# The last image's gate stage in a four-layer convolution kernel: channel mean by norm groups, one DFT row spread to all partitions, normed image made ahead

## The chip, the cores and the metric

The kernel runs on one core of one Trainium2 chip. A core has five engines, each with its own instruction queue that is worked in order: TensorE (PE; its weight loads are listed apart as PEld), VectorE (DVE), ScalarE (ACT), GpSimd (POOL) and SyncE (SP, which here only issues transfers). On-chip memory has 128 partitions; matrix products are written to PSUM. The metric is the device time of one execution in microseconds (us). All data are fp32.

## The reference

The input is x of shape (4, 256, 56, 56). Four layers follow each other, each of the form x + layer(group norm of x), with 32 groups of 8 channels. Layers 0 and 2 are involutions (a 7x7 filter made per pixel), layer 1 is a pair of 3x3 convolutions, layer 3 is a gate by Fourier transforms. Only layer 3 is touched:

```python
cf = jnp.fft.fft2(x, axes=(-2, -1)).real.mean(axis=(-2, -1))
cf = jax.nn.sigmoid(cf @ W.T + b)
x_cft = x * cf[:, :, None, None]
sf = jnp.fft.fft2(x.mean(axis=1, keepdims=True), axes=(-2, -1)).real.mean(axis=1)
x_sft = x * sf[:, None, :, :]
return x_cft + x_sft
```

The x in these lines is already the group norm of x; call it xn. The mean of a two-dimensional DFT is the value at the origin, so cf is a sigmoid of W times xn at pixel (0, 0), one number per channel. sf is the real part of the DFT of the channel mean m of xn, one 56x56 plane per image: cos·m·cos − sin·m·sin. The output is x + xn·(cf + sf).

## The kernel before

Channels lie on partitions, in two blocks cb = 0 and 1 of 128 channels; an image block is a tile `xs` of 128 partitions by 3136 pixels. The kernel is written as one program; `in_order` fixes each engine's order to the order in which the instructions are written. Layers 0 and 2 share `involution_layer`. For each of the 8 units (image b, block cb) it runs a tap stage (`tap_matrices`: TensorE L471, evacuated to `kt` by VectorE at L489 and by ScalarE at L482) and then 7 column stages (`apply`: TensorE L513, combined by ScalarE L528 and VectorE L533, and added into the image by VectorE L540). Smaller jobs are hung into the tap stage as `hooks` by number, or behind a column stage as `early` and `late` lists.

Layer 3 rides on layer 2. For images 0 to 2 its work is hung into later units: `channel_mean`, `gate_factors`, and `gate_chunk` (on GpSimd, 14 chunks an image). For the last image there is no later unit for block 1, so the end of `involution_layer` does this in turn:

- the last column's statistics (L844), then `norm_steps`: L194 aggregates, TensorE L197 averages the means over groups, L200 to L205 make the variance, TensorE L208 averages it, L138 and GpSimd's power L139 make `rstd`, L212 makes `shift`;
- `channel_mean(3, 1)`: L574 takes pixel (0, 0); L593 and L596 multiply the image by rstd/256 (32 equal columns, seven chunks of 448 pixels in four column groups), ScalarE L604 adds the shift's mean, L607 writes the mean to DRAM and L608 reads it back as 56 rows on 56 partitions (`m2_of`);
- `gate_factors(3)`: L616 loads w3, L623 and the sigmoid L630 make `cf`, L639 and L649 make the first half of the DFT in `half` (128 partitions x 56);
- `last_gates`: for each of seven chunks of 8 image rows, eight products L700 make sf on all 128 partitions at once. The weights are one column of `half` repeated 128 times, the moving operand is the 56-column table `cs2_sb`. ScalarE L710 makes xn in one of three `gx` buffers, VectorE L713 multiplies it by (sf + cf), GpSimd (block 0) or VectorE (block 1) adds it to `xs` at L715, and L716 stores it, from GpSimd's queue or from SP's.

`dead(b, cb, at, n)` gives scratch room in an image block that is no longer needed; for the last image it is a spare block. `two_banks` hands out PSUM in four pairs of banks, in rotation; `one_bank` is the first of a pair.

Of the kernel before, what the change touches and what calls it, by code (L numbers as in the profile page):

```python
# [10 lines left out]
F32 = mybir.dt.float32  # L11
AF = mybir.ActivationFunctionType
ALU = mybir.AluOpType
# [3 lines left out]
P = 128  # L17
B, C, H, W = 4, 256, 56, 56
NB = C // P
# [7 lines left out]
CR = 8  # L27
NCHUNK = H // CR
# [37 lines left out]
def run(g):  # L66
    for _ in g:
        pass
# [3 lines left out]
def net_kernel(  # L72
# [111 lines left out]
    norms = [[[norm_sb[:, i, b, k, :] for k in range(2)] for b in range(B)] for i in range(4)]  # L184
# [57 lines left out]
    def involution_layer(layer, xin, xout, red, span, sb, xs_of, ahead=None, pending=None):  # L242

        with ExitStack() as es:
# [29 lines left out]
            z_sb = wpool.tile([P, G // 2, ZN], F32, name="z_sb")  # L274
# [67 lines left out]
            strip_sb = wpool.tile([P, HS, QX], F32, name="strip_sb")  # L342
# [214 lines left out]
            def gx_tile():  # L557
                return work.tile([P, CR * W], F32, name="gx", bufs=3)

            def dead(b, cb, at, n):  # L560

                if b < B - 1:
                    return xs_of[b, cb][:, at : at + n]
                if None not in xs_of:
                    xs_of[None] = new_block()
                return xs_of[None][:, at : at + n]
# [121 lines left out]
                nc.gpsimd.dma_start(ov[b, cb][:, at], xs)  # L688
                yield

            def last_gates(b):

                rstd, shift = norms[3][b]
                for j in range(NCHUNK):
                    at = slice(j * CR * W, (j + 1) * CR * W)
                    sf = one_bank()[:, : CR * W]

                    for r in range(CR):
                        y = j * CR + r
                        nc.tensor.matmul(  # L700
                            sf[:, r * W : (r + 1) * W],
                            half[:, y : y + 1].to_broadcast([P, P]),
                            cs2_sb,
                            start=True,
                            stop=True,
                        )
                    for cb in range(NB):
                        xs = xs_of[b, cb][:, at]
                        xn = gx_tile()
                        nc.scalar.activation(  # L710
                            xn, xs, AF.Identity, bias=shift[:, cb : cb + 1], scale=rstd[:, cb : cb + 1]
                        )
                        nc.vector.scalar_tensor_tensor(xn, sf, cf_of[b][:, cb : cb + 1], xn, ALU.add, ALU.mult)  # L713
                        eng = nc.vector if cb == 1 else nc.gpsimd
                        eng.tensor_tensor(xs, xs, xn, ALU.add)  # L715
                        (nc.sync if cb == 1 else nc.gpsimd).dma_start(ov[b, cb][:, at], xs)  # L716


            def step(g):
# [63 lines left out]
            for u, (b, cb) in enumerate(units):  # L783
                hooks = hooks0 if u == 0 else {}
                if prev is not None:
                    pb, pc, st, last_sums = prev
                    hooks.setdefault(1, []).append(last_column(last_sums))
                    place(hooks, norm_of(layer + 1, pb, pc, st), (2, 6, 7, 11, 12, 13))
                    if layer == 2 and u < 3:
                        g = norm_of(2, B - 1, u - 1, pending[1][u - 1])  # L790
                        place(hooks, g, (19, 20, 22, 23, 25, 26))
                    if layer == 2:
                        place(hooks, channel_mean(pb, pc), (13, 17))
                        if pc == 1:
# [48 lines left out]
                def column_sums(tx, st=st, img=img):  # L843
                    nc.vector.bn_stats(st[:, tx, :], img[:, :, tx * TX : (tx + 1) * TX])  # L844

                if ahead is not None and u == len(units) - 1:
                    late[0].append(ahead)

                for tx in range(NTX):
                    for f in early[tx]:  # L850
                        f()
                    apply(b, cb, kt, tx, xws[u * NTX + tx])
                    next_windows()
                    next_strip()
                    if tx > 0:
                        column_sums(tx - 1)
                    for f in late[tx]:
                        f()
                if layer == 0 or b + 1 < B:
                    (nc.gpsimd if layer == 0 else nc.sync).dma_start(xout[b][cb], xs_of[b, cb])  # L860
                prev = b, cb, st, column_sums
            b, cb, st, last_sums = prev
            last_sums(NTX - 1)
            run(norm_of(layer + 1, b, cb, st))
            if layer == 2:
                factors = gate_factors(b)
                run(channel_mean(b, cb))
                for _ in range(4):
                    next(factors)
                last_gates(b)  # L870
            in_order(since)
# [596 lines left out]
```

## Time and profile before

| | before |
|---|---|
| time, median of 3 | 1877.03 us (1874.28 to 1877.57) |
| profiled span | 1872.6 us |
| PE busy | 1709.5 us (91%), 24030 instructions |
| DVE busy | 1433.3 us (77%) |
| ACT busy | 748.8 us (40%) |
| POOL busy | 432.2 us (23%) |
| last image write by L540 ends | 1820.6 us |
| first POOL add L715 starts | 1842.66 us |
| last POOL store L716 is issued by | 1865.13 us |

The profile is one execution. A line of a group reads: line, engine, operation, output<-inputs with their shapes (for a product the first pair is rows by columns of the weights), count | busy us, mean ns of one | idle us of the engine just before, and who released it. A line of the timeline reads: start in us, duration in us, engine, line, operation, count, and in brackets the idle time before it with its releaser. An fp32 product shows as two matmul records. PEclk is the clock that TensorE was granted, as a share of full speed. Matmul ends are modelled, so a busy PE is not PE at its peak.

### The profile page before, as it was taken

To read this page: it belongs to the slowest core of one execution; us is meant where nothing else is said; L and a number is where in the kernel's file an instruction comes from. 1 tells how busy PE (TensorE), PEld (TensorE's weight loads), DVE (VectorE), ACT (ScalarE), POOL (GpSimd) and SP (SyncE) were. 2 spreads that over 40 slices of the span, in tenths; PEclk is the share of its full clock that TensorE was granted. 3 is DMA by queue.
4 is the path that set the end of the run, shared out by engine and by line. 5 is a ranking of instruction groups with operands and counts; after the bars stand their busy time and mean duration, and the time that the engine had idled before them with its cause. 6 is when DMAs were issued, how large, how long until landed. Compare 5 with 4: busy or idle time off the path is not lost.

```text
span 1872.6 us, 55573 instructions
## 1 busy us (share of the span) xinstructions
PE 1709.5 (91%) x24030; PEld 1509.6 (81%) x24030; DVE 1433.3 (77%) x2823; ACT 748.8 (40%) x1657; POOL 432.2 (23%) x615
## 2 busy tenths in 40 slices
PE   5999999999759999999999999997999898898866
PEld 3888888888748988898899889885877777778865
DVE  5687777876678988898888988865767777777763
ACT  2445445454423222232223212114666565565532
POOL 2323433244210000000000000000000581681672
PEclk9999999999979999999999999998999999999995
DMA  3445544453533111110111210223533764773652
GB/s 97 150 146 177 153 120 140 152 153 111 160 121 100 42 60 61 61 67 36 62 58 57 73 35 33 89 76 89 174 107 132 231 193 147 222 215 105 177 147 76
DMA packets 65589, 215.72 MB, mean 115 GB/s; under 512 B 13564, under 2 KB 20528, under 8 KB 61504
## 3 DMA queue, kind: packets, MB, share of 16 engines
q1 hardware_dynamic: 44448, 141.62, 24.1%
q0 software_dynamic: 14848, 65.85, 10.9%
q10 hardware_dynamic: 6048, 4.68, 0.8%
q8 instruction: 190, 3.11, 0.7%
q14 instruction: 55, 0.45, 0.1%
HBM read 76.24 MB, written 49.16 MB: 67 GB/s over the span
## 4 chain that ended last, share of the span: by engine, by line
PE 65%; DVE 21%; DMA 5%; POOL 3%; issue 3%; ACT 2%; SPq 1%; POOLq 0%; ACTq 0%; DVEq 0%
PE mm L1242 20%; PE ps L513 14%; DVE kt L489 12%; PE mm L1160 10%; PE ps L471 7%; PE mm L1131 6%; PE ps L381 4%; DMA xw<-xw 3%; PE ps L433 2%; DVE un L533 2%; PE ps L700 1%; ACT hp L452 1%; PE ps L596 1%; DVE st L844 1%; DMA xs<-in_x_dram 1%
## 5 line engine op out<-in xcount | busy, mean ns | idle before, releaser
L513 PE MATMUL ps<-kt,xw 126*32 126x48 f32 (+1 forms) x12544 | 383.5, 236 | 56.9 <-DMA xw<-xw 21.3
L513 PEld LDWEIGHTS ps<-kt,xw 126*32 126x32 f32 (+1 forms) x12544 | 344.2, 122 | 102.4 <-issue 48.1
L471 PE MATMUL ps<-hp,z_sb 64*126 64x133 f32 x6144 | 389.0, 282 | 19.2 <-DVE kt L489 7.0
L471 PEld LDWEIGHTS ps<-hp,z_sb 64*126 64x126 f32 x6144 | 370.7, 189 | 34.1 <-DVE kt L489 8.7
L489 DVE TENSOR_TENSOR kt<-ps,zb_sb 126x798 f32<-126x798 f32 x384 | 357.9, 978 | 43.6 <-PE ps L471 43.1
L1242 PE MATMUL mm<-v,u_sb 128*128 128x280 f32 (+1 forms) x1728 | 384.9, 384 | 3.3 <-DVE v L1067 3.3
L1242 PEld LDWEIGHTS mm<-v,u_sb 128*128 128x128 f32 x1728 | 327.6, 190 | 57.8 <-DVE v L1067 3.6
L482 ACT ACTIVATE kt<-ps,zb_sb 126x133 f32<-126x133 f32 x768 | 224.0, 441 | 179.4 <-PE ps L471 179.4
L1160 PE MATMUL mm<-v,u_sb 128*128 128x252 f32 (+1 forms) x936 | 211.2, 386 | 12.6 <-DVE v L1051 12.6
L1160 PEld LDWEIGHTS mm<-v,u_sb 128*128 128x128 f32 x936 | 177.2, 190 | 42.9 <-issue 12.6
L533 DVE SCALAR_TENSOR_TENSOR un<-ps,par_sb,un 128x240 f32<-128x240 f32 x224 | 98.4, 457 | 103.1 <-ACT un L526 98.8
L533 DVE SCALAR_TENSOR_TENSOR un<-ps,s,un 128x240 f32<-128x240 f32 x224 | 102.3, 457 | 92.9 <-ACT un L528 88.7
L1279 POOL DMA_DIRECT2D x<-xs x24 | 13.1, 546 | 684.9 <-DVE xs L1278 539.5
L1227 ACT ACTIVATE res<-xs,shift,norm_sb 128x1120 f32<-128x1120 f32 (+1 forms) x24 | 30.2, 1260 | 235.2 <-DVE xs L1278 119.7
L538 POOL TENSOR_TENSOR xs<-un,xs 128x240 f32<-128x240 f32 x112 | 72.4, 665 | 224.2 <-DVE un L533 224.1
L382 ACT COPY xw<-ps 126x896 f32<-126x896 f32 x112 | 101.5, 907 | 49.6 <-PE ps L381 39.2
L381 PE MATMUL ps<-ident_sb,strip_sb 128*126 128x128 f32 x784 | 111.4, 282 | 1.6 <-DVE kt L489 0.8
L526 ACT ACTIVATE un<-ps,par_sb 128x240 f32<-128x240 f32 x112 | 50.1, 448 | 138.6 <-PE ps L513 136.7
L1131 PE MATMUL mm<-xs,u_sb 128*128 128x126 f32 (+1 forms) x792 | 98.3, 277 | 1.3 <-DVE xs L1094 1.0
L528 ACT ACTIVATE un<-ps,bn_t,s 128x240 f32<-128x240 f32 x112 | 60.1, 538 | 97.8 <-PE ps L513 93.7
L139 POOL TENSOR_TENSOR norm_sb<-norm_sb,mhalf 128x1 f32<-128x1 f32 x32 | 19.2, 602 | 341.7 <-DVE norm_sb L138 341.7
L1131 PEld LDWEIGHTS mm<-xs,u_sb 128*128 128x128 f32 x792 | 94.3, 191 | 2.7 <-issue 1.4
(194 smaller groups left out, 1973.0 us busy)
## 6 DMA issues: line engine op xcount, KB each, us to landing
xw<-xw SPq DMA_DIRECT2D x168, 252.0 KB
xw<-xw SPq DMA_DIRECT2D x224, 126.0 KB
xw<-xw POOLq DMA_DIRECT2D x56, 252.0 KB, 4.7
xs<-x SPq DMA_DIRECT2D x24, 560.0 KB
x<-xs POOLq DMA_DIRECT2D x8, 1568.0 KB, 7.9
xs<-x SPq DMA_DIRECT2D x8, 1568.0 KB
xs<-in_x_dram SPq DMA_DIRECT2D x6, 1568.0 KB
x<-xs SPq DMA_DIRECT2D x6, 1568.0 KB
```

Of the source, the lines that this page charges most:

```text
L381: nc.tensor.transpose(ps[:Q, k * P : (k + 1) * P], flat[:, k * Q : (k + 1) * Q], ident_sb)
L382: nc.scalar.copy(xw[:, :NSB, :], ps[:Q, : NSB * P].rearrange("q (n c) -> q n c", n=NSB))
L471: nc.tensor.matmul(ps[:Q, i, k * NT : (k + 1) * NT], z_sb[i * R : (i + 1) * R, cb * GB // 2 + gp, z0 : z0 + Q], hp[i * R : (i + 1) * R, py ...
L482: nc.scalar.activation(kt[:, g0 + i, pb, :, k], ps[:Q, i, k * NT : (k + 1) * NT], AF.Identity, bias=zb_sb[:, cb * GB + g0 + i, p0 + k : p0 ...
L489: nc.vector.tensor_tensor(kt[:, g0 : g0 + 2, pb], ps[:Q, :, : PB * NT].rearrange("q i (k t) -> q i t k", k=PB), zb_sb[:, cb * GB + g0 : cb ...
L513: nc.tensor.matmul(v[m * j : m * j + m, i, :, k * TP : (k + 1) * TP], xw[:, window(ty), m * j : m * j + m], kt[:, ng * j : ng * j + ng, :, ...
L528: nc.scalar.activation(part, o[0], AF.Identity, bias=bn["t4"][:, cb : cb + 1], scale=bn["s4"][ng][:, 0, cb : cb + 1])
L533: nc.vector.scalar_tensor_tensor(part, o[e], s, part, ALU.mult, ALU.add)
L538: nc.gpsimd.tensor_tensor(dst, u, dst, ALU.add)
L1131: nc.tensor.matmul(ps[:, co * m : (co + 1) * m], u[ci][:, co * P : (co + 1) * P], v2[:, e, : n // 2, ci * WT : (ci + 1) * WT], start=(ci = ...
L1160: nc.tensor.matmul(ps, u1_sb[:, ci, dy, k, co * P : (co + 1) * P], v[:, k, dy * NB + ci : (dy + n - 1) * NB + ci + 1 : NB, :], start=(j == 0),
L1242: nc.tensor.matmul(ps, u2_sb[:, ci, dy, k, co * P : (co + 1) * P], v[:, k, dy * NB + ci : (dy + n - 1) * NB + ci + 1 : NB, :], start=(j == 0),
```

## The change

Only the last image is treated differently. For its block 1:

- `last_mean` takes the channel mean without transfers. For each of the 56 image columns x, a product with weights `xs[:, :, x]` (128 channels x 56 rows) and 16 moving columns of the averaging table gives the mean of each group of 8 channels, with the image row on the partition. These sums don't need the norm, which is applied afterwards: `rstd` of each group is spread over the partitions by one product, the sums are multiplied by it (`parts`) and reduced over the groups, and the mean of `shift` is added. The result is written straight to `m2_of[1]`.
- `norm_steps` is interleaved with it: the 56 products stand first in TensorE's order, the norm's two products behind them.
- `gate_factors(3)` starts at hook 20 of the last tap stage, so that w3 is loaded there.
- `last_normed` makes xn for the whole image ahead of the gates, for block 0 in the buffer of h, for block 1 in three `gx` buffers and in room that is free by then.
- `last_gates` makes sf once by one product (56x56), spreads its rows by a mask into `rows` (partition y holds row y in slot y mod 8, zeros elsewhere), and one product a chunk with a selecting weight brings the chunk's eight rows to all 128 partitions. `last_ones` makes mask and selector from the identity at hook 22.
- for block 1, VectorE multiplies by (sf + cf + 1/rstd), and ScalarE adds −shift/rstd, which gives x + xn·(cf + sf) without a VectorE addition.

```diff
+            def last_ones():
+                by = ident_sb[:, : CR * CR]
+                for i, axes in enumerate(("p (j r) -> p r j", "p (j r) -> p j r")):
+                    last_xn[i] = dead(B - 1, NB - 1, 6 * CR * W + 128 + i * CR, CR)
+                    nc.vector.tensor_reduce(last_xn[i], by.rearrange(axes, r=CR), mybir.AxisListType.X, ALU.add)
+            def last_normed(b, cb):
...
+                for j, xn in enumerate(pieces):
+                    last_xn[j, cb] = xn
+                    nc.scalar.activation(xn, xs_of[b, cb][:, j * n : (j + 1) * n], AF.Identity,
+                        bias=shift[:, cb : cb + 1], scale=rstd[:, cb : cb + 1])
+                    yield
+            def last_mean(b, bank):
+                cb, ng = NB - 1, P // 8
+                xs = xs_of[b, cb].rearrange("p (h w) -> p w h", w=W)
+                rstd, shift = (t[:, cb : cb + 1] for t in norms[3][b])
+                by = gavg_sb.rearrange("p (g i) -> p i g", i=8)[:, 0, :]
...
+                for x in range(W):
+                    nc.tensor.matmul(means[:, x // m, x % m, :], xs[:, x, :], by, start=True, stop=True)
+                yield
+                nc.tensor.matmul(bank[:H, 1 : 1 + ng], rstd.to_broadcast([P, H]), by, start=True, stop=True)
+                scales = dead(b, cb, 4 * CR * W + NB * C, 32)[:H]
+                yield
+                nc.tensor.matmul(
+                    bank[:H, 1 + ng : 2 + ng], shift.to_broadcast([P, H]), cmean[:, 0:1], start=True, stop=True)
+                nc.vector.tensor_scalar(first_of[b][:, cb : cb + 1], xs[:, 0, 0:1], rstd, shift, ALU.mult, ALU.add)
+                nc.vector.tensor_scalar_mul(scales[:, :ng], bank[:H, 1 : 1 + ng], 8.0 / C)
+                parts = dead(b, cb, 2 * CR * W, 2 * CR * W)[:H].rearrange("y (i x g) -> y i x g", i=2, g=ng)
+                nc.vector.tensor_tensor(parts, means,
+                    scales[:, :ng].unsqueeze(1).unsqueeze(1).to_broadcast([H, 2, m, ng]), ALU.mult)
+                nc.vector.tensor_copy(scales[:, ng : ng + 1], bank[:H, 1 + ng : 2 + ng])
+                nc.vector.tensor_reduce(
+                    m2_of[cb].rearrange("y (i x) -> y i x", i=2), parts, mybir.AxisListType.X, ALU.add)
+                nc.vector.tensor_scalar_add(m2_of[cb], m2_of[cb], scales[:, ng : ng + 1])
+                yield
             def last_gates(b):
...
+                nc.vector.reciprocal(inv, rstd[:, 1:2])
+                nc.vector.tensor_add(cfx, cf_of[b][:, 1:2], inv)
+                nc.vector.scalar_tensor_tensor(back, shift[:, 1:2], -1.0, inv, ALU.mult, ALU.mult)
+                ps = one_bank()
+                nc.tensor.matmul(ps[:H, :W], half, cs2_sb, start=True, stop=True)
+                rows = dead(b, NB - 1, 0, CR * W)[:H]
+                nc.vector.tensor_tensor(
+                    rows.rearrange("y (r w) -> y r w", r=CR),
+                    ps[:H, :W].unsqueeze(1).to_broadcast([H, CR, W]),
+                    last_xn[0][:H].unsqueeze(2).to_broadcast([H, CR, W]), ALU.mult)
                 for j in range(NCHUNK):
                     at = slice(j * CR * W, (j + 1) * CR * W)
                     sf = one_bank()[:, : CR * W]
-                    for r in range(CR):
-                        y = j * CR + r
-                        nc.tensor.matmul(sf[:, r * W : (r + 1) * W],
-                            half[:, y : y + 1].to_broadcast([P, P]), cs2_sb, start=True, stop=True)
+                    nc.tensor.matmul(sf, last_xn[1][:H, j : j + 1].to_broadcast([H, P]), rows, start=True, stop=True)
                     for cb in range(NB):
-                        xs = xs_of[b, cb][:, at]
-                        xn = gx_tile()
-                        nc.scalar.activation(
-                            xn, xs, AF.Identity, bias=shift[:, cb : cb + 1], scale=rstd[:, cb : cb + 1])
-                        nc.vector.scalar_tensor_tensor(xn, sf, cf_of[b][:, cb : cb + 1], xn, ALU.add, ALU.mult)
-                        eng = nc.vector if cb == 1 else nc.gpsimd
-                        eng.tensor_tensor(xs, xs, xn, ALU.add)
-                        (nc.sync if cb == 1 else nc.gpsimd).dma_start(ov[b, cb][:, at], xs)
+                        xs, xn = xs_of[b, cb][:, at], last_xn[j, cb]
+                        f = cfx if cb == 1 else cf_of[b][:, cb : cb + 1]
+                        nc.vector.scalar_tensor_tensor(xn, sf, f, xn, ALU.add, ALU.mult)
+                        if cb == 0:
+                            nc.gpsimd.tensor_tensor(xs, xs, xn, ALU.add)
+                            nc.gpsimd.dma_start(ov[b, cb][:, at], xs)
+                        else:
+                            nc.scalar.activation(xs, xn, AF.Identity, bias=back)
+                            nc.sync.dma_start(ov[b, cb][:, at], xs)
...
+                        elif pb == B - 1:
+                            factors = gate_factors(pb)
+                            place(hooks, factors, (20,))
+                            hooks.setdefault(22, []).append(last_ones)
...
-            run(norm_of(layer + 1, b, cb, st))
+            if layer == 0:
+                run(norm_of(layer + 1, b, cb, st))
             if layer == 2:
-                factors = gate_factors(b)
-                run(channel_mean(b, cb))
-                for _ in range(4):
+                run(last_normed(b, 0))
+                bank = one_bank()
+                mean, norm = last_mean(b, bank), norm_steps(st, lambda: bank, 3, b, cb)
+                next(mean)
+                for _ in range(5):
+                    next(norm)
+                next(mean)
+                next(norm)
+                next(mean)
+                normed = last_normed(b, cb)
+                for _ in range(2):
+                    next(normed)
+                next(factors)
+                run(normed)
+                for _ in range(2):
                     next(factors)
                 last_gates(b)
```

More of the change, by code (lines that the diff above doesn't have):

```diff
@@ L689, in gate_chunk @@
                 yield
+            last_xn = {}
+            def last_ones():
[4 more added lines that the diff above has]
+            def last_normed(b, cb):
+                rstd, shift = norms[3][b]
+                n = CR * W
+                if cb == 0:
+                    h = new_h()
+                    pieces = [h[:, j * n : (j + 1) * n] for j in range(NCHUNK)]
+                else:
+                    z = z_sb.rearrange("p g z -> p (g z)")
+                    pieces = [z[:, k * n : (k + 1) * n] for k in range(2)]
+                    pieces += [strip_sb.rearrange("p h w -> p (h w)")[:, :n], dead(b, cb, n, n)]
+                    pieces = [gx_tile() for _ in range(NCHUNK - len(pieces))] + pieces
+                for j, xn in enumerate(pieces):
+                    last_xn[j, cb] = xn
+                    nc.scalar.activation(
+                        xn,
+                        xs_of[b, cb][:, j * n : (j + 1) * n],
+                        AF.Identity,
+                        bias=shift[:, cb : cb + 1],
+                        scale=rstd[:, cb : cb + 1],
+                    )
+                    yield
@@ new lines, in last_mean @@
+            def last_mean(b, bank):
[3 more added lines that the diff above has]
+                by = gavg_sb.rearrange("p (g i) -> p i g", i=8)[:, 0, :]
+                m = W // 2
+                pair = two_banks()
+                means = pair[:H, :, : m * ng].rearrange("y i (x g) -> y i x g", g=ng)
+                for x in range(W):
[5 more added lines that the diff above has]
+                nc.tensor.matmul(
+                    bank[:H, 1 + ng : 2 + ng], shift.to_broadcast([P, H]), cmean[:, 0:1], start=True, stop=True
+                )
+                nc.vector.tensor_scalar(first_of[b][:, cb : cb + 1], xs[:, 0, 0:1], rstd, shift, ALU.mult, ALU.add)
+                nc.vector.tensor_scalar_mul(scales[:, :ng], bank[:H, 1 : 1 + ng], 8.0 / C)
+                parts = dead(b, cb, 2 * CR * W, 2 * CR * W)[:H].rearrange("y (i x g) -> y i x g", i=2, g=ng)
+                nc.vector.tensor_tensor(
+                    parts,
+                    means,
+                    scales[:, :ng].unsqueeze(1).unsqueeze(1).to_broadcast([H, 2, m, ng]),
+                    ALU.mult,
+                )
+                nc.vector.tensor_copy(scales[:, ng : ng + 1], bank[:H, 1 + ng : 2 + ng])
+                nc.vector.tensor_reduce(
+                    m2_of[cb].rearrange("y (i x) -> y i x", i=2), parts, mybir.AxisListType.X, ALU.add
+                )
+                nc.vector.tensor_scalar_add(m2_of[cb], m2_of[cb], scales[:, ng : ng + 1])
+                yield
@@ L691, in last_gates @@
             def last_gates(b):
                 rstd, shift = norms[3][b]
+                inv = small.tile([P, 1], F32, name="inv", bufs=1)
+                nc.vector.reciprocal(inv, rstd[:, 1:2])
+                cfx = small.tile([P, 1], F32, name="cfx", bufs=1)
+                nc.vector.tensor_add(cfx, cf_of[b][:, 1:2], inv)
+                back = small.tile([P, 1], F32, name="back", bufs=1)
+                nc.vector.scalar_tensor_tensor(back, shift[:, 1:2], -1.0, inv, ALU.mult, ALU.mult)
@@ L694, in last_gates @@
+                ps = one_bank()
+                nc.tensor.matmul(ps[:H, :W], half, cs2_sb, start=True, stop=True)
+                rows = dead(b, NB - 1, 0, CR * W)[:H]
+                nc.vector.tensor_tensor(
+                    rows.rearrange("y (r w) -> y r w", r=CR),
+                    ps[:H, :W].unsqueeze(1).to_broadcast([H, CR, W]),
+                    last_xn[0][:H].unsqueeze(2).to_broadcast([H, CR, W]),
+                    ALU.mult,
+                )
                 for j in range(NCHUNK):
@@ L696, in last_gates @@
                     sf = one_bank()[:, : CR * W]
-                    for r in range(CR):
-                        y = j * CR + r
[L700 to L706, printed above, removed]
-                    for cb in range(NB):
-                        xs = xs_of[b, cb][:, at]
-                        xn = gx_tile()
[L710 to L713, printed above, removed]
-                        eng = nc.vector if cb == 1 else nc.gpsimd
-                        eng.tensor_tensor(xs, xs, xn, ALU.add)
-                        (nc.sync if cb == 1 else nc.gpsimd).dma_start(ov[b, cb][:, at], xs)
+                    nc.tensor.matmul(sf, last_xn[1][:H, j : j + 1].to_broadcast([H, P]), rows, start=True, stop=True)
+                    for cb in range(NB):
+                        xs, xn = xs_of[b, cb][:, at], last_xn[j, cb]
+                        f = cfx if cb == 1 else cf_of[b][:, cb : cb + 1]
+                        nc.vector.scalar_tensor_tensor(xn, sf, f, xn, ALU.add, ALU.mult)
+                        if cb == 0:
+                            nc.gpsimd.tensor_tensor(xs, xs, xn, ALU.add)
+                            nc.gpsimd.dma_start(ov[b, cb][:, at], xs)
+                        else:
+                            nc.scalar.activation(xs, xn, AF.Identity, bias=back)
+                            nc.sync.dma_start(ov[b, cb][:, at], xs)
             def step(g):
```

## The prediction

> **What bounds the kernel now.** The change touches only the last column block of the last image (image 3, channels 128 to 255) and what follows it, so I read the whole-kernel shares once (TensorE 91% busy) and then only the end. The timeline of the last 55 us, cut to the hand-overs:
>
> ```profile
> 1820.53 1.15 DVE L844 BATCH_NORM_STATS2 st<-xs 128x6 f32<-128x448 f32 x2
> ...
> 1822.20 0.56 PE L197 MATMUL ps<-mv,gavg_sb 128*128 128x1 f32 x2 [3.81 <-DVE mv L194]
> ...
> 1824.52 0.56 POOL L139 TENSOR_TENSOR norm_sb<-norm_sb,mhalf 128x1 f32<-128x1 f32 x1 [5.86 <-DVE norm_sb L138]
> ...
> 1826.12 3.21 PE L596 MATMUL ps<-xs,mean 128*32 128x448 f32 x14
> ...
> 1832.51 0.32 SPq L608 DMA_DIRECT2D m<-m  x1
> 1832.89 0.84 SPq L616 DMA_DIRECT2D xs<-in_w_dram  x2
> 1835.09 1.87 PE L623 MATMUL ps<-first,xs 128*128 128x1 f32 x8 [5.75 <-DMA xs<-in_w_dram]
> ```
>
> This is a strictly serial preamble: the last image write ends at 1820.6 (the L540 just ahead of the statistics), then norm, channel mean, a trip of the mean through DRAM (L607, L608, about 2.5 us from 1830.0), the late load of w3 (TensorE waits 5.75 us), the gate factors. Then comes the steady part, by groups with shapes kept apart, 1836 to 1866 us:
>
> ```profile
> L700 PE MATMUL ps<-cs_sb,half 128*128 128x56 f32 x112 | 24.1, 420 | 0.6 <-ACT gx L710 0.6
> L700 PEld LDWEIGHTS ps<-cs_sb,half 128*128 128x128 f32 x112 | 24.0, 333 | 0.8 <-ACT gx L710 0.8
> L710 ACT ACTIVATE gx<-xs,norm_sb 128x448 f32<-128x448 f32 x14 | 9.9, 752 | 14.5 <-POOL xs L715 14.5
> L713 DVE SCALAR_TENSOR_TENSOR gx<-ps,cf,gx 128x448 f32<-128x448 f32 x14 | 8.9, 678 | 10.1 <-ACT gx L710 5.2 <-PE ps L700 4.9
> L715 POOL TENSOR_TENSOR xs<-xs,gx 128x448 f32<-128x448 f32 x7 | 7.8, 1121 | 26.2 <-DVE gx L713 26.2
> L715 DVE TENSOR_TENSOR xs<-xs,gx 128x448 f32<-128x448 f32 x7 | 7.5, 1071 | 0.2
> L716 POOL DMA_DIRECT2D out_dram<-xs x7 | 3.9, 561 | 2.1 <-POOL xs L715 2.1
> ```
>
> TensorE issues L700 without a gap: 24.1 us over 7 chunks is 3.44 us a chunk, and ScalarE, VectorE and GpSimd all wait. The first POOL add starts at 1842.66, its seventh store is issued at 1865.13, and the closing drain and semaphores take the span to 1872.6 (7.5 us). The granted clock, by windows:
>
> ```profile
> 1801.30:1804.70 3.40, 1.23 (x72) 1.02 (x72) 2.14 (x4) 0.55 (x1) 3.10 (x5) 1.00 0.87 254
> 1804.70:1808.10 3.40, 3.40 (x34) 3.05 (x31) 1.35 (x3) 1.43 (x2) 3.02 (x4) 0.51 0.42 125
> 1808.10:1811.50 3.40, 3.40 (x118) 3.17 (x118) 1.50 (x4) 1.07 (x2) 3.18 (x6) 0.99 0.73 209
> ...
> 1818.40:1821.80 3.40, 0.00 (x0) 0.00 (x0) 3.23 (x9) 0.52 (x1) 0.27 (x1) 1.00 0.18 67
> 1821.80:1825.20 3.40, 1.11 (x4) 1.00 (x4) 1.13 (x7) 0.00 (x0) 0.56 (x1) 0.51 0.00 0
> 1838.50:1848.70 10.20, 10.20 (x50) 10.20 (x49) 4.68 (x6) 3.67 (x6) 3.39 (x4) 0.50 0.13 51
> ```
>
> After "core 0" the columns are PE, PEld, DVE, ACT, POOL busy, then clock, DMA share, GB/s. A thin 3.4 us stretch is followed by one at half clock, a full one by full clock; and L700, though gapless, stays at 0.50. So the whole tail runs at half clock.
>
> **What the Trainium skill says.** (1) "TensorE: Matmul & The Clock Gate", LDWEIGHTS: the load's time goes with the number of columns, not with the contraction. The trace agrees at half clock: L700 (128 columns) steps by 24.1/112 = 0.215 us, L639 (56 columns) by about 0.09 to 0.13:
>
> ```profile
> 1836.89 0.34 PE L639 MATMUL ps<-cs_sb,m 56*56 56x56 f32 x1
> ...
> 1837.02 0.30 PE L639 MATMUL ps<-cs_sb,m 56*56 56x56 f32 x1
> ...
> 1837.11 0.30 PE L639 MATMUL ps<-cs_sb,m 56*56 56x56 f32 x1
> ...
> 1837.20 0.30 PE L639 MATMUL ps<-cs_sb,m 56*56 56x56 f32 x1
> ```
>
> (2) Same page, Part 1: activity is judged over free-running windows of about 3.4 us. The trace agrees (changes at 1804.7, 1808.1, 1821.8). (3) "SBUF — State Buffer", Door 1: an access that goes to a new 16-byte line every time pays a penalty. The new weights are read at a step of 56 floats; no run here shows such weights, which is my largest unknown. (4) Same page, "Who interferes with whom": a VectorE instruction with two SBUF inputs and a GpSimd one that reads SBUF exclude each other. The trace agrees: L715 on VectorE starts at 1843.20 under the POOL L715 that ends at 1843.79, and ends at 1844.26, 0.47 us after it.
>
> **The change, part by part.**
>
> *Ahead of the tail.* The w3 load moves to hook 20 of the last tap stage, where SP has nothing urgent; it costs nothing there and removes the 5.75 us wait. Two small reductions (`last_ones`) go into the same stage on VectorE, which is gapless there (L489). The nearest row, L164, takes 0.28 us over 128 elements; these have 64, so about 0.15 each: **+0.3 us**.
>
> *Channel mean by norm groups.* 56 products (weights 128x56 strided, 16 moving columns) start when the last image write is done, 1820.67. Each fp32 product is two records (56 L700 calls are 112 records), so 112 records. Priced low by L639, 0.09 us, which gives 10.1; priced high by L700's 0.215, which gives 24.1. I take 0.10 us, 11.2 us, less 0.8 us because the full clock lasts until 1821.8: **10.4 us, ending 1831.1**. The clock then falls: the moving part is 16 columns to 56 loaded, thinner than L700's 56 to 128, which never lifted it. In TensorE's queue the norm's L197 stands behind all of this; VectorE's aggregate is ready at 1822.05 and waits 9 us. That is the new wait.
>
> *Norm.* L197's start to the end of L139's power was 1822.17 to 1825.08: 2.9 us, to **1834.0**.
>
> *Rest of the mean, no DRAM.* From that power: the rstd product and its landing 0.55; scales 0.2; `parts`, 56x896 from PSUM. From L489 (798 elements, 0.976) and L533 (240, 0.457), slope 0.93 ns an element, so 1.07; copy 0.16; the reduce over 896 the same 1.07; add 0.17; gaps 0.15. Sum 3.4. `first` and the shift fit within the 0.55.
>
> *Gate factors.* L623 (1.87 us) and the sigmoid lie beside VectorE's 2.5 us of parts and reduce. On the path: L639 0.65 with its hand-over 0.75, L649 0.44 with its own 0.55. Three [P,1] operations (0.16 each) lie beside the spreading DFT product (0.4 with hand-over): 0.6. `rows` (448 from PSUM, by the same slope 0.65): 0.65. First wide product: two records of 448 columns; L596 took 3.21 us for 14 records in four column groups, about 0.75 a record at half clock, so 1.5, with load and landing 1.8. First VectorE product 0.68, hand-over 0.1. Sum from the power: 3.4 + 0.75 + 0.55 + 0.6 + 0.65 + 1.8 + 0.78 = 8.5. **First POOL add at 1842.5**, almost where it was: the saved DRAM and w3 waits are paid back to the mean products and the norm behind them.
>
> *Normed image made ahead.* Seven ScalarE activations (0.7 each) for channels 0 to 127 fall into its idle stretch from 1819.0 to 1829.4, at nothing; the seven others follow the power, two before the sigmoids, and chunk 0 and 1 are ready 6 us before use. Writing into h, z_sb, the strip and the dead block waits for nobody: their last readers (L471, L381) ended over 10 us before.
>
> *Gates.* Per chunk: TensorE 1.5 us instead of 3.44; VectorE 2 x 0.678 = 1.36 (its add is gone, ScalarE does 0.7 instead); GpSimd as before 1.12 add + 0.30 wait + 0.56 store issue = 1.98, about 2.03 with its queue's semaphore. **GpSimd becomes the bound**: 7 x 2.03 = 14.2 us. The stores (3.2 MB in some 14 us, 230 GB/s) are under the 254 GB/s seen at 1801. End of issue 1842.5 + 14.2 = 1856.7 against 1865.13: 8.4 us less; with +0.3, **8.1 us less: 1877.0 − 8.1 = 1869**. The closing 7.5 us stay.
>
> **The rivals.**
>
> *A, the forecast:* POOL-paced end, mean products at about 0.10 us. **1869**, chance 0.60.
>
> *B, the mean products keep the full clock.* For it: only 2.3 us of idle go ahead of them. Against: the L700 clock. 112 x 0.06 = 6.7 us, 3.7 less: **1865**, chance 0.12.
>
> *C, the strided weights cost half as much again* (0.15 us, 16.8 us, +6.4): **1875**, chance 0.12. For a moderate penalty only: L513's moving operand comes in runs of 3 floats, and its 112 records still take only 3.2 to 3.3 us.
>
> *D, they cost twice or more*, as if 128 columns were loaded: 112 x 0.215 = 24.1, +13.7. The gates' gain and more is lost in front of the norm: **1883**, slower, chance 0.16. For it: every one of the 56 weight columns is in another line. Against: at half clock each column already has about 1.7 ns (0.095 us over 56).
>
> **How the numbers follow.** Predicted: A. Low end 1863.5 takes in B and a little; the high end 1877 takes in C and stops short of D (0.16 left out, 0.03 at the low end). Faster by over 0.2% is below 1873.3: A, B, and a little of C, with something of A lost: 0.75. Slower by over 0.2%, above 1880.8: 0.15. The rest, 0.10.
>
> **What would show it.** Mean products: 112 records from 1820.7 to about 1831, clock 0.5 after the first microsecond; L197 right behind them. POOL adds every 2.0 us with no idle between, TensorE and VectorE waiting on free banks or each other. First POOL add within 1.5 us of 1842.7. It is wrong if the products' spacing is not 0.10, if the POOL adds are spaced by TensorE (more than 2.1 us), or if the closing stretch after the last store grows beyond 7.5 us.

## The result, and the profile after

| | before | changed |
|---|---|---|
| time, median of 19 runs each | 1876.55 us | 1868.59 us |
| ratio, 95% interval | 1 | 0.9952 (0.994 to 0.9965) |
| end of the last image write (L540) to the first GpSimd add | 22.06 us | 20.19 us |
| first GpSimd add to the last store issued (the gates) | 22.47 us | 14.12 us |
| last store issued to the end of the span (the close) | 7.47 us | 7.44 us |
| sum: last image write to the end | 52.00 us | 41.75 us |

The forecast was 1869. The last four rows come from one profile of each. They are the better ruler: the seven column stages of the last unit alone, ahead of the last image write, took 35.0 to 40.1 us from profile to profile of the kernels below, in no order that follows the edits. Single times therefore scatter (1861.41 to 1873.01 us for the changed kernel) by far more than the intervals of medians. The close is nearly all one drain on GpSimd that starts with its last store: 7.27 us before and after.

The stretch from the image write to the first add, called the preamble below, has a scatter of its own. In the five profiles that keep TensorE's order up to the first add (the two of the changed kernel and, below, e4, e9 and e10) it is 20.19 to 21.33 us, and the whole difference is how far ahead of the image write the mean products begin (3.05 to 1.92 us). From the first mean product to the first add all five take 23.2 us.

The timeline of the changed kernel from the mean products to the third GpSimd instruction of the gates (start, duration, engine, line; in brackets the idle time before, with its releaser):

```profile
1814.70 11.75 PE L735 MATMUL ps<-gavg_sb,xs 128*56 128x16 f32 x112
...
1817.38 0.37 DVE L540 SCALAR_TENSOR_TENSOR xs<-un,xs 128x208 f32<-128x208 f32 x1
...
1818.85 0.34 DVE L194 BATCH_NORM_AGGREGATE mv<-st 128x2 f32<-128x42 f32 x1
1826.38 0.50 PEld L197 LDWEIGHTS ps<-mv,gavg_sb 128*128 128x128 f32 x2
...
1828.68 0.56 POOL L139 TENSOR_TENSOR norm_sb<-norm_sb,mhalf 128x1 f32<-128x1 f32 x1 [13.38 <-DVE norm_sb L138]
...
1837.94 1.13 POOL L789 TENSOR_TENSOR xs<-xs,hp 128x448 f32<-128x448 f32 x1 [8.71 <-DVE hp L787]
...
1839.37 0.58 POOL L790 DMA_DIRECT2D out_dram<-xs  x1 [0.30 <-DVE hp L787]
...
1839.97 1.15 POOL L789 TENSOR_TENSOR xs<-xs,hp 128x448 f32<-128x448 f32 x1
```

The statistics are aggregated at 1819.19, and the norm's first product starts at 1826.38: 7.2 us behind the mean products. In the gates GpSimd goes from store issue to next add without idle time. By groups, shapes kept apart, 1836 to 1853 us:

```profile
L783 PE MATMUL ps<-xs 56*128 56x448 f32 x14 | 10.8, 960 | 1.1 <-ACT xs L715 1.1
L789 POOL TENSOR_TENSOR xs<-xs,hp 128x448 f32<-128x448 f32 x7 | 8.0, 1140 | 8.8 <-DVE hp L787 8.7
L787 DVE SCALAR_TENSOR_TENSOR hp<-ps,cf,hp 128x448 f32<-128x448 f32 x7 | 4.8, 685 | 3.3 <-PE ps L783 3.3
...
L790 POOL DMA_DIRECT2D out_dram<-xs x7 | 3.9, 561 | 2.1 <-POOL xs L789 0.9 <-DVE hp L787 0.6 <-DVE gx L787 0.3
```

Where L700 took 24.1 us before, the wide product L783 takes 10.8. GpSimd's add has 8.8 us of idle time, 8.7 of them ahead of the first; its 8.0 + 3.9 + 2.1 us fill the 14.1 of the gates. The wait of the first L783 is put down to ScalarE's norm image (L715), but that isn't what bounds the preamble: e10 below makes no image ahead and takes the same 23.2 us from the first mean product to the first add.

### The profile page after: what moved, and what is told of

Read it like the earlier page. It is cut to its first block, busy times and chain, and to the rows that moved or that the text cites. A ratio compares the mean times of both kernels' runs of the same rounds, so it can differ in the third digit from the quotient of the medians.

```text
span 1859.5 us, 55572 instructions
## 1 busy us (share of the span) xinstructions
PE 1705.2 (92%) x24028; PEld 1501.5 (81%) x24028; DVE 1430.2 (77%) x2824; ACT 751.4 (40%) x1662; POOL 432.0 (23%) x615
## 4 chain that ended last, share of the span: by engine, by line
PE 67%; DVE 20%; DMA 4%; issue 3%; POOL 3%; ACT 2%; SPq 0%; DVEq 0%; POOLq 0%; ACTq 0%
PE mm L1336 20%; PE ps L513 15%; DVE kt L489 11%; PE mm L1254 10%; PE ps L471 8%; PE mm L1225 6%; PE ps L381 4%; DMA xw<-xw 2%; PE ps L433 2%; DVE un L533 2%; ACT hp L452 1%; DMA gx<-x 1%; PE ps L783 1%; DVE st L925 1%; DMA xs<-in_x_dram 1%
## 5 line engine op out<-in xcount | busy, mean ns | idle before, releaser
L513 PE MATMUL ps<-kt,xw 126*32 126x48 f32 (+1 forms) x12544 | 385.2, 236 | 57.0 <-DMA xw<-xw 19.2
L513 PEld LDWEIGHTS ps<-kt,xw 126*32 126x32 f32 (+1 forms) x12544 | 345.9, 122 | 102.6 <-issue 47.8
```

The lines of the kernel that those rows point to most:

```text
L513: nc.tensor.matmul(v[m * j : m * j + m, i, :, k * TP : (k + 1) * TP], xw[:, window(ty), m * j : m * j + m], kt[:, ng * j : ng * j + ng, :, ...
```

## The experiments

My theory: TensorE's eight products a chunk bounded the gates and GpSimd bounds them now; the preamble stayed long because the norm waits behind the mean products. The rivals: the gain lies in the mean without transfers; the gates are bound by stores or VectorE; the strided weights are the cost. All the figures of the table are from one profile a kernel, in us. Kernels e5, e9 and e10 were run once, so only their profiles are used:

| kernel | image write to first add | gates | close | sum |
|---|---|---|---|---|
| before | 22.06 | 22.47 | 7.47 | 52.00 |
| changed, first and second profile | 20.19, 20.74 | 14.12, 14.11 | 7.44, 7.52 | 41.75, 42.37 |
| e1 eight products again | 21.27 | 22.48 | 7.50 | 51.25 |
| e2 mean by DRAM | 18.57 | 14.12 | 7.50 | 40.19 |
| e3 norm between the products | 19.10 | 14.13 | 7.50 | 40.73 |
| e4 fewer chunks on GpSimd | 21.33 | 10.96 | 7.23 | 39.52 |
| e5 contiguous weights | 16.96 | 14.13 | 7.51 | 38.60 |
| e6 wide product alone | 21.51 | 15.74 | 7.44 | 44.69 |
| e7 products spread | 12.96 | 14.13 | 7.50 | 34.59 |
| e24 = e2 and e4 | 18.52 | 10.97 | 7.22 | 36.71 |
| e74 = e7 and e4 | 12.96 | 10.96 | 7.20 | 31.12 |
| e9 w3 late | 20.95 | 14.12 | 7.43 | 42.50 |
| e10 norm image in the gates | 20.90 | 18.26 | 7.49 | 46.65 |

### e1: the eight products a chunk again

```diff
...
-                    nc.tensor.matmul(sf, last_xn[1][:H, j : j + 1].to_broadcast([H, P]), rows, start=True, stop=True)
+                    for r in range(CR):
+                        y = j * CR + r
+                        nc.tensor.matmul(sf[:, r * W : (r + 1) * W], half[:, y : y + 1].to_broadcast([P, P]), cs2_sb, start=True, stop=True)
```

> The changed kernel with one part undone: each chunk of the gates takes its sf from eight products with weights 128x128 and 56 moving columns again, without mask and rows; the mean, the early norm image and ScalarE's addition stay. The measure is the stretch from the end of the last image write (L540) to the end of the span: 52.0 us before, 41.8 after. Theory (the product per chunk had been the bound, GpSimd is the bound now): TensorE spaces the chunks by 3.44 us again, GpSimd idles 1.4 us a chunk, the first GpSimd add comes about where it was (the DFT product, rows and the wide product, some 3 us, go, and 3.5 us for the first eight products come), so 6 x (3.44 - 2.02) = 8.5 us longer: 50 us, and the kernel's time within 0.2% of before. Rival (the gain came from the mean without transfers and the normed image ahead, and the gates are bound by stores or VectorE): at most 2 us longer, 44 us.

The DFT product, the mask and `rows` go with it. Measured: ratio 1.0002 (0.9988 to 1.0015), so no gain is left that the times can show; in the profile 0.75 us are. By groups, 1836 to 1865 us:

```profile
L776 PE MATMUL ps<-cs_sb,half 128*128 128x56 f32 x112 | 24.1, 420 | 0.5 <-DVE half L649 0.5
...
L788 POOL TENSOR_TENSOR xs<-xs,hp 128x448 f32<-128x448 f32 x7 | 7.9, 1122 | 17.7 <-DVE hp L786 17.7
```

GpSimd idles 17.7 us instead of 8.8, 9.0 of them ahead of the first chunk and the rest between chunks. The theory's 50 us were 51.25; the rival's were 44 at most.

### e6: the wide product alone, in the kernel before

```diff
-                    for r in range(CR):
...
+                    nc.tensor.matmul(sf, ones[1][:H, j : j + 1].to_broadcast([H, P]), rows, start=True, stop=True)
```

> The kernel before with one part of the change done alone: the DFT is made once and one wide product a chunk spreads eight rows to all partitions; the mean by DRAM, the late w3, the norm image in the chunks and VectorE's addition stay as before. TensorE then needs 1.5 us a chunk. Theory (behind the products, VectorE and GpSimd come next: VectorE's two products of 0.68 us and an addition that waits for GpSimd's, 1.07 us, are 2.4 us a chunk): chunks at 2.4 to 2.6 us, the stretch from the last image write to the end about 46 us against 52.0 before and 41.8 in the changed kernel. Rival (three gx buffers and ScalarE hold the chunks near the old pace): above 3 us a chunk and 49 us or more. If 2.03 us a chunk and 43 us, ScalarE's addition and the norm image ahead were worth nothing.

Measured: ratio 0.997 (0.9952 to 0.9988), sum 44.69. This one edit is worth 7.3 of the 10 us. The timeline in the gates:

```profile
1855.44 1.07 DVE L725 TENSOR_TENSOR xs<-xs,gx 128x448 f32<-128x448 f32 x1
...
1856.44 1.26 DVE L723 SCALAR_TENSOR_TENSOR gx<-ps,cf,gx 128x448 f32<-128x448 f32 x2
```

VectorE has no gap and the chunks are 2.29 us apart (1.26 for its two products, the rest for an addition that runs partly under GpSimd's). Next behind TensorE came VectorE, at a slightly better pace than expected (2.4 to 2.6).

### e10: the norm image in the gates again

```diff
-                        xs, xn = xs_of[b, cb][:, at], last_xn[j, cb]
+                        xs, xn = xs_of[b, cb][:, at], gx_tile()
+                        nc.scalar.activation(xn, xs, AF.Identity, bias=shift[:, cb : cb + 1], scale=rstd[:, cb : cb + 1])
...
-                run(last_normed(b, 0))
...
```

> The changed kernel with the norm image made in the gates again, chunk by chunk in three gx buffers, by ScalarE. Theory (in ScalarE's order the next chunk's norm stands behind this chunk's last addition, which waits for VectorE, so the latencies add up: 0.7 + 0.7 + 0.68 + 0.67 and hand-overs): 2.8 to 3.0 us a chunk, gates of 19 us against 14.1, the stretch to the end 46 to 47 us. Rival (ScalarE's throughput counts, 2.1 us a chunk): gates of 14.5 to 15 us, so the norm image ahead would be worth under 1 us.

Measured: chunks 2.72 us apart, gates 18.26, sum 46.65.

```profile
1849.67 0.67 ACT L795 ACTIVATE xs<-gx,back 128x448 f32<-128x448 f32 x1 [0.75 <-DVE gx L790]
1850.24 1.40 ACT L786 ACTIVATE gx<-xs,norm_sb 128x448 f32<-128x448 f32 x2
...
1851.02 0.68 DVE L790 SCALAR_TENSOR_TENSOR gx<-ps,cf,gx 128x448 f32<-128x448 f32 x1 [1.39 <-ACT gx L786]
```

ScalarE is busy 2.0 of 2.72 us; the rest is its wait for VectorE, with the next chunk's norm behind the waiting instruction. So ScalarE's addition pays only together with the norm image ahead: with the addition and without the image the gates are slower (18.26 us) than in e6 (15.74), which has neither.

### e4: three of GpSimd's seven chunks to ScalarE and SP

```diff
+                        onto = cb == 0 and j % 2 == 0
...
-                        if cb == 0:
+                        if onto:
                             nc.gpsimd.tensor_tensor(xs, xs, xn, ALU.add)
...
```

> The changed kernel with three of GpSimd's seven chunks (1, 3, 5 of block 0) made as block 1's are: ScalarE adds the bias, SP stores. Theory (GpSimd's 2.02 us a chunk is the bound of the gates): the chunks are spaced by TensorE's wide product, 1.49 us, all seven take 10.5 instead of 14.1 us, and the stretch to the end falls by 3.2 us to 38.5. Rival (stores are the bound, 3.2 MB over the last 12 us, or VectorE): no change within 0.7 us, as the same bytes and the same VectorE products remain.

Measured: gates 10.96 instead of 14.12, that is 3.16 us less; ratio 0.9946 (0.9926 to 0.9965), which the times can't tell from the changed kernel's. By groups, 1843 to 1856 us:

```profile
L782 PE MATMUL ps<-xs 56*128 56x448 f32 x13 | 9.9, 951 | 0.0
L789 POOL TENSOR_TENSOR xs<-xs,hp 128x448 f32<-128x448 f32 x4 | 4.5, 1124 | 11.7 <-DVE hp L787 11.7
```

The bytes and the VectorE products are the same, so neither bounded the gates: GpSimd did. TensorE, without a gap, now sets the pace. The sum fell by only 2.2 us in this profile because the preamble was 1.1 longer; there the mean products began 1.92 us ahead of the image write instead of 3.05.

### e2: the mean by DRAM again, the rest as changed

```diff
-                mean, norm = last_mean(b, bank), norm_steps(st, lambda: bank, 3, b, cb)
...
+                run(norm_of(3, b, cb, st))
+                run(channel_mean(b, cb))
```

> The changed kernel with the other part undone: the mean of the last block goes through DRAM again, after the norm, w3 stays early and the new gates stay. Theory (the preamble is serial either way, and the mean products in front of the norm cost what the transfers cost): norm 4.5 us after the last image write, mean products 3.5, ScalarE's copies 1.2, two transfers about 4.4, then 5.1 to the first GpSimd add, which is 19 us after the last image write, against 20.2 in the changed kernel; the stretch to the end 41 us, that is the same or 1 us shorter. Rival (the transfers were the costly part, so taking them out is worth some us): first GpSimd add 22 us after the last image write, as it was before, and the stretch 44 us or more.

Measured: first add at 18.57, sum 40.19; ratio 0.9923 (0.9896 to 0.9951). With the transfers back the kernel is no slower: the mean without transfers is a loss of 1.6 us, or of 2.2 against the second profile. TensorE waits for the transfers like this:

```profile
1832.44 0.34 PE L639 MATMUL ps<-cs_sb,m 56*56 56x56 f32 x1 [2.53 <-DMA m<-m]
```

L639 starts 13.4 us after the image write here, and 14.8 in the changed kernel (1832.60 less 1817.75). In the kernel before it starts 16.3 us after it (1836.89 less 1820.60), although the read from DRAM (L608) is issued at the same 11.9 us in both kernels. The difference of 2.9 us is the late w3: before, L639 stands behind L623 on TensorE, which waits for it.

### e3: the norm's products between the mean products

```diff
                 for x in range(W):
+                    if x in (24, 32, 40):
+                        yield
                     nc.tensor.matmul(means[:, x // m, x % m, :], xs[:, x, :], by, start=True, stop=True)
```

> The changed kernel with another order on TensorE: the norm's first product stands after 24 of the 56 mean products, its second after 32, the product that spreads rstd after 40, and the rest follow. Nothing is added or removed. Theory (the norm waits behind the mean products, and this wait is on the path): the norm's 2.9 us and the rstd product come off the path, TensorE ends the mean products at about 12.9 us after their start instead of 11.6, and the first GpSimd add comes 2 to 3 us earlier, 17 to 18 us after the last image write; the stretch to the end 39 us. Rival (another chain, w3's products with the sigmoid or ScalarE's seven activations after the norm, is as long): under 0.7 us.

Measured: first add at 19.10, 1.1 us earlier (1.6 against the second profile), where 2 to 3 were expected; sum 40.73; ratio 0.9947 (0.9925 to 0.9969), which the times can't tell from the changed kernel's. From the first mean product to the first add it is 21.4 us instead of 23.2, so 1.8 less. The norm's 2.9 us came off the path, but its two products lengthen TensorE's row by 1.2 us (1823.06 to 1835.91 is 12.85, against 11.68). In one point the edit was not what was expected: the product that spreads rstd stood behind all 56 products, not after 40. The rest is the scatter: this profile's products began 2.3 us ahead of the image write's end instead of 3.05.

### e7: the mean products spread over the columns

```diff
+                for tx in range(NTX):
+                    ps = one_bank()
+                    for i in range(TX):
+                        if tx == NTX - 1 and i == TX // 2:
+                            yield
+                        nc.tensor.matmul(ps[:H, i * ng : (i + 1) * ng], xs[:, tx * TX + i, :], by, start=True, stop=True)
...
+                    nc.scalar.copy(raw[:, tx * TX * ng : (tx + 1) * TX * ng], ps[:H, : TX * ng])
```

> The changed kernel with the mean products spread: eight products for image columns 8(tx-1) to 8 tx - 1 stand behind column stage tx of the last unit, each set is copied out of PSUM by ScalarE, and only the last column's eight products are left behind the last image write, four between the norm's two products and four after. Same products in number and kind. Theory (the norm's wait behind 56 products is the only thing left in the preamble, and TensorE has idle time in the last columns): power at 4.6 us after the last image write, first GpSimd add 8.7 later, 13.3 us against 20.2; the stretch to the end 35 us, and the columns themselves at most 2 us longer. Rival (TensorE's order in the columns is tight, so 6 x 1.7 us of products push the column stages back by as much): the stretch falls as said, but the last image write comes 6 us or more later and the time is no better than the changed kernel's.

Measured: first add at 12.96, sum 34.59; ratio 0.9912 (0.988 to 0.9943); 13.3 and 35 were expected. TensorE's timeline behind the last image write, which ended at 1823.21:

```profile
1824.71 0.38 PE L197 MATMUL ps<-mv,gavg_sb 128*128 128x1 f32 x2 [1.98 <-DVE mv L194]
1825.02 1.01 PE L737 MATMUL ps<-gavg_sb,xs 128*56 128x16 f32 x8
1825.96 0.59 PE L208 MATMUL ps<-d,gavg_sb 128*128 128x1 f32 x2
```

The norm's product now follows its aggregate at once. The column stages took 39.7 us here and 38.1 in e74, within the 35.0 to 40.1 of the other kernels, so a price of the spread in the columns isn't seen; one below 2 us can't be excluded.

### e5: contiguous weights

```diff
-                    nc.tensor.matmul(means[:, x // m, x % m, :], xs[:, x, :], by, start=True, stop=True)
+                    nc.tensor.matmul(means[:, x // m, x % m, :], xs_of[b, 0][:, x * H : (x + 1) * H], by, start=True, stop=True)
```

> The changed kernel with the 56 mean products reading their weights in contiguous rows of the already finished block 0 instead of columns of block 1 at a step of 56 floats; so the mean is of other data, all else is as it was. In the changed kernel a record took 0.104 us, both in the first 2.5 us at full clock and at half clock after. Theory (the strided read holds each record at about 0.104 us, and half clock nearly hides it): contiguous weights step by 0.05 to 0.07 us while the clock is full and by 0.093 to 0.096 at half clock, and the 112 records take about 9.5 to 10 us instead of 11.65. Rival (0.104 is a fixed price of a pair of load and product, whatever the stride): 11.6 us again, 0.104 in both clocks.

Measured: from the first record to the norm's product 7.7 us (1818.17 to 1825.90) instead of 11.7 (1814.70 to 1826.38), and from there to the first add the same as in the changed kernel. Windows on the mean products alone, changed kernel first, then e5 (after the window: length, busy time and records of PE, then of PEld, clock, DMA share, GB/s):

```profile
1815.00:1816.00 1.00, 1.00 (x12) 1.00 (x11) 1.00 0.19 75
...
1819.00:1820.00 1.00, 1.00 (x13) 1.00 (x12) 0.50 0.00 0
```

```profile
1819.50:1820.50 1.00, 1.00 (x23) 1.00 (x22) 1.00 0.00 0
...
1823.50:1824.50 1.00, 1.00 (x13) 1.00 (x13) 0.50 0.00 0
```

A record that lies across an edge counts on both sides. With its modelled length (0.26 and 0.20 us) taken into account, the steps over longer stretches are 0.103 us for strided weights in both clocks, and 0.052 and 0.093 for contiguous ones. The stride doubles the price at full clock and adds a tenth at half clock. The row took less time than expected largely because the clock stayed full for 3.5 us.

### e9: w3 late

```diff
-                            place(hooks, factors, (20,))
...
+                factors = gate_factors(b)
+                next(factors)
                 run(last_normed(b, 0))
```

> The changed kernel with w3 loaded at the start of the tail, ahead of the norm image of block 0, and not at hook 20 of the tap stage. Theory (with the mean products in front, w3 has 12 us to land where it needs about 3, so the hook is worth nothing here): first GpSimd add at 20.2 to 20.8 us after the last image write and 41.8 to 42.4 to the end, as in the two profiles of the changed kernel. Rival (the wait of 5.75 us before was the load, and it returns in part): L623 waits for the transfer, 22 us or more to the first add.

Measured: first add at 20.95, sum 42.50, against 20.19 and 20.74, 41.75 and 42.37; from the first mean product to the first add the same 23.2. L623 follows L741 without a wait:

```profile
1835.81 0.33 PE L741 MATMUL ps<-cmean,norm_sb 128*56 128x1 f32 x2
1836.07 1.86 PE L623 MATMUL ps<-first,xs 128*128 128x1 f32 x8
```

The early hook is worth nothing in the changed kernel. With the mean by DRAM an early w3 was worth 2.9 us (e2); whether the start of the tail would be early enough there wasn't tried.

### e24, e74 and the changed kernel once more

> Two earlier changes together: the mean by DRAM after the norm (first GpSimd add at 18.6 us after the last image write in its own run) and three of GpSimd's chunks given to ScalarE and SP (gates of 11.0 instead of 14.1 us in its own run). Theory (they lie one after the other on the path and add): 18.6 + 11.0 + 7.3 = 37 us from the last image write to the end, some 3 us shorter than with the mean by DRAM alone. Rival (ScalarE, which then also copies the mean out and makes the norm image late, holds up the first chunks): 38.5 us or more.

Measured: sum 36.71, ratio 0.9937 (0.9904 to 0.9969). The two parts add (37 was expected).

> The version that the runs point to: mean products spread over the last columns and three of GpSimd's chunks given to ScalarE and SP. Theory (the two savings lie one after the other): 13.0 us from the last image write to the first GpSimd add, 11.0 of gates, 7.3 to the close, 31.3 in all against 52.0 before and 41.8 in the changed kernel; with the columns at most 2 us longer, about 1857 us where the kernel before has 1876, and 10 us under the changed kernel. Rival (spread products hold the columns up, or the stores now bind): less than 5 us under the changed kernel.

> The changed kernel itself, to be compared with on the same chip: 41.8 us from the last image write to the end, ratio to before 0.995.

Measured on the same chip: e74 1857.52 us, ratio 0.9905 (0.9882 to 0.9929); the changed kernel 1867.52, ratio 0.996 (0.9946 to 0.9974); before 1875.69. The sum is 31.12 against 42.37. This version beats both kernels: it is 10 us under the changed one, as expected.

## Why the prediction was right, point by point

- **Gates: right, and shown.** GpSimd's pace was put at 2.03 us a chunk and is 2.02 ((1850.07 − 1837.94)/6 by its adds), 14.12 us in all for 14.2. Eight products again (e1) bring 8.4 us back, and three chunks less for GpSimd (e4) take 3.2 away. TensorE's 1.5 is 1.49; it waited for nobody, where the prediction had it wait for banks. The close stayed at 7.44.
- **From the power to the first add: right.** 8.5 forecast, 8.70 measured; the norm 2.9 forecast, 2.87 measured (1826.38 to 1829.25).
- **Start of the mean products: wrong.** The prediction lets them "start when the last image write is done", at 1820.67 (the write ended at 1820.60). But only the products for the last eight image columns need that write. TensorE began as soon as its own last L513 was through, 3.05 us ahead of the write's end (1.9 to 2.5 in other profiles).
- **Price of the mean products: mis-sized.** 10.4 us forecast, 11.7 measured. The 0.8 us taken off for the first microsecond at full clock weren't there: the strided record takes 0.103 us at full clock too, where the contiguous one takes 0.052 (e5). So the penalty of point (3) was real. With it rival B's 0.06 us could not come true even at full clock. Rival D's factor of two does hold at full clock, but most of the products ran at half clock, where the stride costs a tenth.
- **The 0.09 us of L639: the right price, from a reading that doesn't show it.** A second record, with `sin_sb`, starts some 0.01 us after each of those with `cs_sb` (at 1836.90 and 1837.03, for instance), so each step of 0.09 us is that of a pair. The price held all the same: in e5 a single row of contiguous 56-column weights steps by 0.093 us at half clock. Nor could L700 (128 rows by 128 columns) and L639 (56 by 56) tell columns from rows, as point (1) needs. The row of e5 (128 by 56) can: 0.093 against L700's 0.215 us, with the same 128 rows.
- **w3: right that the wait goes, wrong in cause.** The wait of 5.75 us is gone, but not through the hook (e9). Behind 12 us of mean products a load issued at the start of the tail is early enough.
- **"The saved DRAM and w3 waits are paid back to the mean products and the norm behind them": right, and more so than said.** VectorE's aggregate waits 7.2 us for the norm's product (9 forecast), and e2 shows the mean without transfers to be a small loss in this order.
- **The sum, and luck.** 8.1 us forecast; the profiles show 10.25 and, with the second one, 9.6; the ratio's interval is 6.6 to 11.3 us. The products started 1.9 to 3.05 us earlier than forecast, and the stretch from their start to the first add is 23.2 us where 21.8 were forecast. These errors partly cancel: the products ended 8.6 us after the image write, forecast 10.4. That the median lies within half a microsecond of 1869 is luck; that the gates give most of the gain is not. The two reductions of `last_ones` took 0.46 us on VectorE, forecast 0.3; what they cost the kernel is too small to be seen.

The gain of 10.25 us can be laid out in steps: the wide product 7.3 us (e6); w3 early, the norm image ahead and ScalarE's addition together 4.5 (e6 to e2), of which 2.9 lie ahead of the first add and 1.6 in the gates; the mean without transfers −1.6 (e2 to changed).

## What to carry to other kernels

Ask of each part of a change which instruction will stand behind it on its engine: work that is free of a dependency can still bring a loss when the short link of a critical chain is queued behind it. Nearly twelve microseconds of independent products belong where their engine idles, not ahead of the two products that everything waits for. After a bound is removed, compute the next engine's time per step, GpSimd's own store issue and its wait for the add included, since it is often close below.

## What the runs showed of the hardware that was not expected

In these profiles fp32 weights read at a step of 56 floats (56 columns) took 0.103 us a record at full and at half clock; contiguous ones of the same shape took 0.052 and 0.093 (e5).

For the products of this tail, issue without a gap did not keep the full clock, nor bring it back. In the seven profiles that have the mean products L735 in one row (the two of the changed kernel, e1, e4, e5, e9, e10), the clock fell from 1.00 to 0.50 between 2.3 and 5.5 us after the first record: 2.6 in the changed kernel's first profile, 3.5 in e5. L700 stayed at 0.50 for its 24.1 us and L783 for its 10.8. What decides it isn't shown. L735 and L700 load more columns than they move (56 to 16, 128 to 56), but L783 moves more than it loads (448 to 128).
